# Cross-attention with text keys on one core: the loads of x move from SyncE's queue to GpSimd's

## The chip, the cores and the metric

One core of a Trainium2 chip runs the whole kernel. Time is device microseconds of one execution, lower is better; verdicts compare medians of several runs of both kernels on one chip. The engines are TensorE (PE, its weight loads shown as PEld), VectorE (DVE), ScalarE (ACT), GpSimd (POOL) and SyncE (SP), which here only issues DMAs.

## The reference

Every batch of 512 queries attends over 77 text keys, with 20 heads of 32 columns. The other three attentions of the module (object, others, image prompt) get slices of the keys that are empty for a context of 77 rows, so only the text part counts, all in float32:

```python
q = _heads(hidden_states @ to_q_w)                       # x: (32, 512, 640)
h_txt = _sdpa(q, _heads(ehs_txt @ to_k_w), _heads(ehs_txt @ to_v_w))
out = _merge(h_txt) @ to_out_w + to_out_b + hidden_states
```

where `_sdpa` is softmax(q kT / sqrt(32)) v for each head.

## The kernel before

Each float32 operand of a matmul is kept as a rounded high part and a low part, and each product is done as three passes (high x high, high x low, low x high). A first stage (some 280 us) makes keys and values of all batches and puts them into DRAM (`k_dram`, `v_dram`). Then 32 batches are worked through, each in five **slots** (`slot`, L557; n = 5 b + j): slot j takes head group j, four heads, 128 columns. The order in which each engine issues its instructions is the order in which the code calls them; nothing is rescheduled. So a call's place in `slot` is its place in its engine's queue.

What a slot does, with the lines that matter below:

- Scores, in four parts of 128 queries (L368 on PE), then the negated maxima (`nm`, L376 on DVE) and the exponentials with their sums (L386 on ACT).
- `normalize` (L401, POOL) scales the P of the slot before by `rs`, the reciprocal of the sums (L396, DVE). `transpose_p` (L408, DVE) turns it in blocks into `z`, and four stores (L415, SP) put it into a DRAM scratch, `pd`. `load_p` (L424 and L425, SP) reads a `pd` back as `raw`, in the layout that PE needs; there are three slots from a slot's scores to its values.
- `cast_p`, `rest_p` and `last_p` split `raw` into `pp`: L432 and L438 on ACT, L439 on DVE, L446 on POOL. `values` (L460, eight matmuls on PE) then makes P V; its last two matmuls read the rows that L446 writes. `split_a` (L104 on ACT, L105 on DVE) splits the result.
- Queries of the next slot (L333, PE), split by `split_q` (L344 and L348 on ACT, L350 on DVE).
- Pieces of the output projection of the batch before or the one before that (L490, PE). Residual rows are loaded by `load_residual` (L479, SP), get the bias by `add_bias` (L483, POOL), and `finish` (L518 on DVE, L522 on SP) adds and stores them.
- `refill` loads keys and values of a later head group (L310, L313 and L320, SP).

**x.** `load_x` (L262) loads x of a batch into the one buffer `xs`, in four quarters; quarter q goes to partitions 32 q to 32 q + 31, each as 32 partitions x 16 runs of 160 numbers (640 B), 320 KB in all. `transpose_x` (L273, DVE) turns `xs` in place, in four parts, and each part needs all four quarters. `split_x` (L280 on ACT, L281 on POOL) makes the five `xt` tiles of the next batch's queries. Slot j = 4 of batch b loads x of batch b + 2, slots 0 to 2 of batch b + 1 transpose it, slots 2 and 3 split it. The tables that place the parts hold, for each j, three tuples, which `slot` runs ahead of the queries' second half, behind the last scores, and at the end:

```python
TRANSPOSE_X = {0: ((), (0,), ()), 1: ((1,), (2,), ()), 2: ((3,), (), ())}
SPLIT_X = {2: ((0,), (1,)), 3: ((2, 3), (4,))}
```

All DMAs are issued by SP. Each of them waits, by the program's own counters, until the DMA issued eight places before on that queue has landed, besides what its data need.

Of the kernel before, what the change touches and what calls it, by code (L numbers as in the profile page):

```python
# [24 lines left out]
Q = 32  # L25
# [25 lines left out]
def kernel(  # L51
# [25 lines left out]
    nc = tc.nc  # L77
    B, S, C = x.shape
# [180 lines left out]

    xts, raws, pps, ats, xss, pds, sms, pqs, pas, xrs, pos = ({} for _ in range(11))  # L260

    def load_x(b, quarters=range(4)):  # L262

        if b not in xss:
            xss[b] = main.tile([P, S // Q, C // 4], F32, tag="xs", name="xs")
        xs = xss[b]
        src = x[b].rearrange("(a j) (q u) -> q j a u", j=Q, q=4)
        for q in quarters:
            nc.sync.dma_start(xs[q * Q : (q + 1) * Q, :, :], src[q])

    def transpose_x(b, i):
        part = xss[b][:, 4 * i : 4 * i + 4, :].rearrange("p a u -> p (a u)")
# [81 lines left out]
    def scores(n, t):  # L354
        b, j = divmod(n, NC_)
        g = GROUP_OF[j]
        qt, (kb, kc) = qts[n % 2], kbs[g]
        jg = j - GROUPS[g][0]
        sc = ps.tile([P, S], F32, tag="sc", name="sc", bufs=3)
        half = KCOLS // 2  # L360
        for m, (cols, keys_) in enumerate(
            (
                (slice(0, KCOLS), kb[:, jg]),
                (slice(0, half), kc[:, jg, 0]),
                (slice(half, KCOLS), kc[:, jg, 1]),
            )
        ):
            nc.tensor.matmul(  # L368
                sc[:, cols],
                qt[:, m, t * P : (t + 1) * P],  # L370
                keys_,
                start=(m == 0),
                stop=(m == 2),
            )
        nm = main.tile([P, HPC], F32, tag="nm", name="nm", bufs=3)
        nc.vector.tensor_reduce(  # L376
            nm, sc[:, :KCOLS].rearrange("p (h k) -> p h k", k=NKEY), AX.X, ALU.max, negate=True
        )
        return sc, nm

    def exps(n, t, sc, nm):
        if t == 0:
            sms[n] = main.tile([P, NQ * HPC], F32, tag="sm", name="sm", bufs=2)
        for i in range(HPC):
            at = t * HPC + i
            nc.scalar.activation(  # L386
                pnb[n % 2][:, at, :NKEY],
                sc[:, i * NKEY : (i + 1) * NKEY],
                AF.Exp,
                bias=nm[:, i : i + 1],  # L390
                accum_out=sms[n][:, at : at + 1],
            )

    def sums(n):
        rs = main.tile([P, NQ * HPC], F32, tag="rs", name="rs", bufs=2)
        nc.vector.reciprocal(rs, sms.pop(n))  # L396
        return rs

    def normalize(n, rs):
        pf = pnb[n % 2][:, :, :NKEY]  # L400
        nc.gpsimd.tensor_tensor(  # L401
            pf, pf, rs.unsqueeze(2).to_broadcast([P, NQ * HPC, NKEY]), ALU.mult
        )
# [24 lines left out]
    def cast_p(n):  # L428

        raw = raws[n]  # L430
        pp = late[0].tile([P, 5, S], FPR, tag="pp", name="pp", bufs=1)
        nc.scalar.copy(pp[:, 0:2, :], raw[:, 0:2, :])  # L432
        pps[n] = pp

    def rest_p(n):

        raw, pp = raws[n], pps[n]
        nc.scalar.copy(pp[:64, 4, :], raw[:64, 2, :])  # L438
        nc.vector.tensor_tensor(  # L439
            pp[:, 2:4, :], raw[:, 0:2, :], pp[:, 0:2, :].bitcast(F32), ALU.subtract  # L440
        )

    def last_p(n):

        raw, pp = raws.pop(n), pps[n]
        nc.gpsimd.tensor_tensor(  # L446
            pp[64:, 4, :], raw[:64, 2, :], pp[:64, 4, :].bitcast(F32), ALU.subtract
        )
# [33 lines left out]
    def add_bias(b, t):  # L482
        nc.gpsimd.tensor_tensor(xrs[b, t], xrs[b, t], bias, ALU.add)  # L483
# [49 lines left out]
    PIECES = {2: (1, 0), 3: (1, 2), 4: (1, 4), 0: (2, 6), 1: (2, 8)}  # L533
    RESIDUAL = {1: (1, 0), 2: (1, 1), 3: (1, 2), 4: (1, 3)}
    BIAS = {2: (1, 0), 3: (1, 1), 4: (1, 2), 0: (2, 3)}
    TRANSPOSE_X = {0: ((), (0,), ()), 1: ((1,), (2,), ()), 2: ((3,), (), ())}
    SPLIT_X = {2: ((0,), (1,)), 3: ((2, 3), (4,))}
    wos = []

    def take(m):  # L540
        values(m)
        split_a(m)

    def refill(b, j, part):

        heads = range(2 * part, 2 * part + 2)
        segments = SEGMENTS[4 * part : 4 * part + 4]
        if j == 0:
            load_keys(b, 1, heads)
        elif j == 1:  # L550
            load_values(b, 0, segments)
        elif j == 2 and b + 1 < B:
            load_keys(b + 1, 0, heads)
        elif j == 3:
            load_values(b, 1, segments)

    def slot(n, beside=None):  # L557
        b, j = divmod(n, NC_)
        ahead, more = n + 1 < N, b + 1 < B
        back, first = PIECES[j]  # L560
        bo_, has_out = b - back, b >= back
        xsplits = SPLIT_X.get(j, ((), ())) if more else ((), ())
        turns = TRANSPOSE_X.get(j, ((), (), ())) if more else ((), (), ())
        taken, second = takes.get(n), seconds.get(n)

        refill(b, j, 0)
        if taken is not None:
            cast_p(taken)
        s = scores(n, 0)
        if taken is not None:  # L570
            rest_p(taken)
        if n:
            normalize(n - 1, sums(n - 1))
        if taken is not None:
            last_p(taken)
        exps(n, 0, *s)
        if ahead:
            queries(n + 1, 0, 2)
        s = scores(n, 1)
        if n - LAG + 1 in pds and n > LATE:  # L580
            load_p(n - LAG + 1)
        refill(b, j, 1)
        finish()
        if j == 4 and b + 2 < B:
            load_x(b + 2, (0, 1))
        if j in RESIDUAL and b >= RESIDUAL[j][0]:
            load_residual(b - RESIDUAL[j][0], RESIDUAL[j][1])
        if j in BIAS and b >= BIAS[j][0]:
            add_bias(b - BIAS[j][0], BIAS[j][1])
        exps(n, 1, *s)  # L590
        for i in turns[0]:
            transpose_x(b + 1, i)
        if ahead:
            queries(n + 1, 2, NC_)
        s = scores(n, 2)
        if n:
            transpose_p(n - 1)
        if ahead:
            split_q(n + 1)
        exps(n, 2, *s)  # L600
        if j == 4 and b + 2 < B:
            load_x(b + 2, (2, 3))
        for c in xsplits[0]:
            split_x(b + 1, c)
        if has_out:
            piece(bo_, first)
        if taken is not None:
            values(taken)
        if beside:
            beside()  # L610
        s = scores(n, 3)
        finish()
        for i in turns[1]:
            transpose_x(b + 1, i)
        if taken is not None:
            split_a(taken)
        for c in xsplits[1]:
            split_x(b + 1, c)
        exps(n, 3, *s)
        if has_out:  # L620
            piece(bo_, first + 1)
        for i in turns[2]:
            transpose_x(b + 1, i)
        if second is not None:
            cast_p(second)
            rest_p(second)
            last_p(second)
            take(second)
            if second + 2 in pds and second + 2 not in takes.values():
                load_p(second + 2)  # L630
# [66 lines left out]

    with tc.manual_schedule(engines=ENGINES):
        g0, gn = GROUPS_KV[-1]
        load_x(0)  # L700
        load_keys(0, 0)
        for h in range(2):
            context_values(g0, gn, 0, h, psv)
        for i in range(NQ):
            transpose_x(0, i)
        for c in range(NC_):
            split_x(0, c, nc.gpsimd if c % 2 else nc.vector)
        load_x(1)
        for t0 in (P, 2 * P):
            for h in range(2):  # L710
                context_values(g0, gn, t0, h, psv)
        queries(0, 0, NC_)
        split_q(0)
        for n in range(LATE):
            slot(n, (lambda: context_values(g0, gn, 3 * P, n // 2, psv)) if n % 2 else None)
        psv.release()
        kvp.release()
        late.append(ctx.enter_context(tc.tile_pool(name="late", bufs=1, reuse_waits="tile")))
        late.append(
            ctx.enter_context(tc.tile_pool(name="psl", bufs=1, space=PSUM, reuse_waits="tile"))  # L720
        )
        load_p(0)
        load_p(1)
        wos.append(late[0].tile([P, NC_, 2, C], FPR, name="wo_s"))
        for n in range(LATE, LATE + 4):
            slot(n)
            for k in {LATE: (0, 1), LATE + 1: (2, 3), LATE + 2: (4,)}.get(n, ()):
                nc.sync.dma_start(wos[0][:, k].bitcast(F32), wo_dram[:, k].bitcast(F32))
        for n in range(LATE + 4, N):
            slot(n)  # L730
        end()
# [40 lines left out]
```

## Time and profile before

| what | us |
|---|---|
| median of 3 runs (lowest, highest) | 2010.02 (2009.55, 2010.04) |
| the profiled execution | 1996.0 |
| its span | 1994.2 |
| DMA, moved in the span | 423.54 MB, mean 212 GB/s |
| POOL L401, 160 times | 364.4 busy, 2277 ns each |
| POOL L446, 160 times | 209.4 busy, 1309 ns each |
| DVE L273, 128 times | 106.5 busy, 834 ns each |
| loads of x, 128 of 320 KB | 7.0 from issue to landing (median) |

The page's parts are read in this order: busy time and span, then what each engine waits for, then the timelines of a stretch. A wait is told as "engine tile line <- releaser": total us, number of times, longest. In a timeline each line has start, duration, engine, source line, operation and tiles (out<-in); the number in brackets is the engine's idle time before it and what ended it. PE's granted clock is 1.00 in every 100 us window from 450 us on, so a slot's length there is PE's own work and its waits. The timelines below are from 1014 to 1048 us, in the middle of the run; a slot j = 0 starts there at 1024.2 and the next at 1034.5.

### The profile page before, as it was taken

Reading aid. Unit: us, or ns where it says so; the run is one execution under the profiler, and the core shown is the slowest. Engines: PE = TensorE matmul, PEld = TensorE weight load, DVE = VectorE, ACT = ScalarE, POOL = GpSimd, SP = SyncE. Lnnn points to the kernel's source line nnn. Section 1 sums busy time; section 2 is a strip of 40 time slices with the busy share of each in tenths; the row PEclk is TensorE's granted clock in tenths of the full one; section 3 lists DMA queues with packets and bytes.
Section 4 is the critical chain, followed back from the end, with each engine's and each line's share of the span. In section 5 each row is a group of like instructions: output and inputs, shape, how many; then the busy total and the mean of one; then the engine's idle time right before and its main releaser. Section 6 shows DMA issues by size and latency. Waiting matters only on the chain.

```text
span 1994.2 us, 38184 instructions
## 1 busy us (share of the span) xinstructions
PE 1950.5 (98%) x11012; PEld 1760.0 (88%) x11012; DVE 1352.5 (68%) x2159; ACT 1598.2 (80%) x6377; POOL 982.8 (49%) x617
## 2 busy tenths in 40 slices
PE   8999997899999999999999999999999999999998
PEld 7889986788899999899899898999989898988997
DVE  4443225777777777777777777777777777777774
ACT  3321128899999999999899999999999899998993
POOL 0000023555555555655556655566655566555554
PEclk9999998999999999999999999999999999999999
DMA  7994366889988889898988899998888888888975
GB/s 172 225 261 107 106 148 146 232 213 232 226 225 226 229 221 231 216 229 212 232 225 224 220 225 230 229 233 222 219 223 223 223 223 225 224 218 230 228 198 164
DMA packets 555997, 423.54 MB, mean 212 GB/s; under 512 B 170192, under 2 KB 459502, under 8 KB 555790
## 3 DMA queue, kind: packets, MB, share of 16 engines
q1 hardware_dynamic: 555789, 421.10, 83.9%
q8 instruction: 91, 1.49, 0.3%
q14 instruction: 117, 0.95, 0.2%
HBM read 245.61 MB, written 175.32 MB: 211 GB/s over the span
## 4 chain that ended last, share of the span: by engine, by line
PE 78%; DMA 9%; SPq 4%; POOL 3%; ACT 2%; issue 2%; DVE 2%; DVEq 0%; ACTq 0%; POOLq 0%
PE po L490 24%; PE pq L333 24%; PE pa L460 13%; PE sc L368 9%; PE pv L197 4%; PE pk L168 4%; DMA raw<-pd 3%; POOL pn L401 2%; DMA pd<-z 2%; SPq L114 1%; DMA xs<-in_x_dram 1%; POOL pp L446 1%; ACT pn L386 1%; DMA k_dram<-ks 1%; DMA cs<-in_ctx_dram 1%
## 5 line engine op out<-in xcount | busy, mean ns | idle before, releaser
L386 ACT ACTIVATE pn<-sc,nm 128x77 f32<-128x77 f32 x2560 | 802.0, 330 | 44.6 <-DVE nm L376 33.8
L401 POOL TENSOR_TENSOR pn<-pn,rs 128x1232 f32<-128x1232 f32 x160 | 364.4, 2277 | 670.3 <-DVE rs L396 643.9
L490 PE MATMUL po<-wo_s,at 128*128 128x320 f32 x3840 | 626.9, 312 | 2.2 <-DVE xr L518 2.2
L333 PE MATMUL pq<-xt,wq_s 128*128 128x512 f32 x2400 | 622.4, 400 | 0.0
L490 PEld LDWEIGHTS po<-wo_s,at 128*128 128x128 f32 x3840 | 566.3, 189 | 2.7 <-DVE xr L518 2.5
L386 ACT ACTIVATION_READ_ACCUMULATOR pn<-sc,nm 128x1 f32 x2560 | 533.1, 208 | 0.0
L333 PEld LDWEIGHTS pq<-xt,wq_s 128*128 128x128 f32 x2400 | 429.6, 190 | 77.4 <-POOL xt L281 0.2
L376 DVE TENSOR_REDUCE nm<-sc 128x4 f32<-128x308 f32 x640 | 294.6, 460 | 298.2 <-PE sc L368 291.0
L460 PE MATMUL pa<-pp,vb 128*128 128x512 f32 x1280 | 334.9, 402 | 18.4 <-ACT pp L432 9.8
L460 PEld LDWEIGHTS pa<-pp,vb 128*128 128x128 f32 x1280 | 243.5, 198 | 62.8 <-POOL pp L446 14.3
L408 DVE STREAM_TRANSPOSE z<-pn 128x1280 f32<-128x1280 f32 x160 | 241.5, 1509 | 36.2 <-POOL pn L401 31.6
L439 DVE TENSOR_TENSOR pp<-raw,pp 128x1024 fp32r<-128x1024 f32 x160 | 196.1, 1226 | 82.4 <-ACT pp L432 72.2
L368 PEld LDWEIGHTS sc<-kc,qt 128*128 128x128 f32 x1280 | 212.8, 189 | 27.2 <-ACT qt L348 4.2
L446 POOL TENSOR_TENSOR pp<-raw,pp 64x512 fp32r<-64x512 f32 x160 | 209.4, 1309 | 37.0 <-ACT pp L438 19.8
L368 PE MATMUL sc<-kc,qt 128*128 128x154 f32 x1280 | 222.9, 255 | 4.5 <-DVE qt L350 3.9
L350 DVE TENSOR_TENSOR qt<-pq,qt 64x512 fp32r<-64x512 f32 x320 | 214.3, 670 | 7.5 <-ACT qt L344 3.1
L281 POOL TENSOR_TENSOR xt<-xs,xt 128x512 fp32r<-128x512 f32 x157 | 200.0, 1296 | 19.4 <-ACT xt L280 12.5
L483 POOL TENSOR_TENSOR xr<-xr,bias 128x640 f32<-128x640 f32 x128 | 201.3, 1573 | 9.7
L348 ACT CAST qt<-qt 64x512 fp32r<-64x512 f32 x320 | 198.8, 621 | 8.9
L368 PE MATMUL sc<-kb,qt 128*128 128x308 f32 x640 | 196.1, 306 | 1.2 <-ACT qt L344 1.2
L432 ACT CAST pp<-raw 128x1024 fp32r<-128x1024 f32 x160 | 170.1, 1063 | 29.7 <-DMA raw<-pd 28.9
L104 ACT CAST at<-pa 128x512 fp32r<-128x512 f32 x160 | 94.9, 593 | 82.2 <-PE pa L460 81.1
(41 smaller groups left out, 1530.8 us busy)
## 6 DMA issues: line engine op xcount, KB each, us to landing
pd<-z SPq DMA_DIRECT2D x640, 160.0 KB, 3.6
raw<-pd SPq DMA_DIRECT2D x160, 512.0 KB, 4.3
xs<-in_x_dram SPq DMA_DIRECT2D x128, 320.0 KB, 7.0
xr<-in_x_dram SPq DMA_DIRECT2D x128, 320.0 KB, 3.8
out_dram<-xr SPq DMA_DIRECT2D x128, 320.0 KB, 3.2
raw<-pd SPq DMA_DIRECT2D x160, 128.0 KB, 4.4
v_dram<-vs SPq DMA_DIRECT2D x19, 640.0 KB, 4.0
k_dram<-ks SPq DMA_DIRECT2D x80, 128.0 KB, 2.4
```

The lines of the kernel that those rows point to most:

```text
L281: engine.tensor_tensor(parts[1], src, parts[0].bitcast(F32), ALU.subtract)
L333: nc.tensor.matmul(pqs[n], wq_s[:, k, a, j * P : (j + 1) * P], xts[b, k][:, c, :], start=(k == 0 and m == 0), stop=(k == NC_ - 1 and m == 2),)
L350: nc.vector.tensor_tensor(qt[r, 1 + w, :], pq[r], qt[r, 0, :].bitcast(F32), ALU.subtract)
L368: nc.tensor.matmul(sc[:, cols], qt[:, m, t * P : (t + 1) * P], keys_, start=(m == 0), stop=(m == 2),)
L376: nc.vector.tensor_reduce(nm, sc[:, :KCOLS].rearrange("p (h k) -> p h k", k=NKEY), AX.X, ALU.max, negate=True)
L386: nc.scalar.activation(pnb[n % 2][:, at, :NKEY], sc[:, i * NKEY : (i + 1) * NKEY], AF.Exp, bias=nm[:, i : i + 1], accum_out=sms[n][:, at : ...
L401: nc.gpsimd.tensor_tensor(pf, pf, rs.unsqueeze(2).to_broadcast([P, NQ * HPC, NKEY]), ALU.mult)
L408: nc.vector.transpose(z.rearrange("p b t j -> p t b j"), pn.rearrange("p (t h) k -> p t (h k)", t=NQ).rearrange("p t (b i) -> p t b i", i=Q),)
L446: nc.gpsimd.tensor_tensor(pp[64:, 4, :], raw[:64, 2, :], pp[:64, 4, :].bitcast(F32), ALU.subtract)
L460: nc.tensor.matmul(pas[n], vb[:, t, :, a], pp[:, c, :], start=(m == 0), stop=(m == len(PASSES) - 1),)
L483: nc.gpsimd.tensor_tensor(xrs[b, t], xrs[b, t], bias, ALU.add)
L490: nc.tensor.matmul(pos[b, t, h][:, :HALF], ats[b * NC_ + j][:, a, t * P : (t + 1) * P], wos[0][:, j, c, h * HALF : (h + 1) * HALF], start= ...
```

## The change

The four quarters of x are issued by POOL (`nc.gpsimd`) in place of SP; only the loads of the first two batches stay on SP. Quarter 0 is issued in slot j = 4 behind `last_p`, quarters 1 and 2 in the same slot behind `add_bias`, quarter 3 in slot j = 0 of the next batch behind `last_p`. Before, quarters 0 and 1 were issued ahead of the residual's load of slot 4, and 2 and 3 behind the third part's exponentials. The first of the four transpositions of x moves from behind the last scores of slot 0 to its end, on DVE from ahead of `split_a`'s L105 to behind it. The computation is the same.

```diff
-    def load_x(b, quarters=range(4)):
+    def load_x(b, quarters=range(4), engine=nc.gpsimd):
...
         for q in quarters:
-            nc.sync.dma_start(xs[q * Q : (q + 1) * Q, :, :], src[q])
+            engine.dma_start(xs[q * Q : (q + 1) * Q, :, :], src[q])
...
-    TRANSPOSE_X = {0: ((), (0,), ()), 1: ((1,), (2,), ()), 2: ((3,), (), ())}
+    TRANSPOSE_X = {0: ((), (), (0,)), 1: ((1,), (2,), ()), 2: ((3,), (), ())}
...
         if taken is not None:
             last_p(taken)
+        if j == 4 and b + 2 < B:
+            load_x(b + 2, (0,))
+        elif j == 0 and b and b + 1 < B:
+            load_x(b + 1, (3,))
         exps(n, 0, *s)
...
         finish()
-        if j == 4 and b + 2 < B:
-            load_x(b + 2, (0, 1))
         if j in RESIDUAL and b >= RESIDUAL[j][0]:
             load_residual(b - RESIDUAL[j][0], RESIDUAL[j][1])
         if j in BIAS and b >= BIAS[j][0]:
             add_bias(b - BIAS[j][0], BIAS[j][1])
+        if j == 4 and b + 2 < B:
+            load_x(b + 2, (1, 2))
         exps(n, 1, *s)
...
         exps(n, 2, *s)
-        if j == 4 and b + 2 < B:
-            load_x(b + 2, (2, 3))
         for c in xsplits[0]:
...
-        load_x(0)
+        load_x(0, engine=nc.sync)
...
-        load_x(1)
+        load_x(1, engine=nc.sync)
```

## The prediction

> **What bounds the kernel now.** First the page's totals.
>
> ```profile
> span 1994.2 us, 38184 instructions
> PE 1950.5 (98%) x11012; PEld 1760.0 (88%) x11012; DVE 1352.5 (68%) x2159; ACT 1598.2 (80%) x6377; POOL 982.8 (49%) x617
> ```
>
> TensorE (PE) is busy 98% of the span, and in the timeline of PE a slot (one head group of one batch) takes 10.3 us, five slots a batch. A change of queues can't shorten a slot whose PE never waits; it can only remove or add PE waits. So the second view is that of PE's waits from 450 to 1900 us, and of its weight loads (PEld):
>
> ```profile
> PE pa L460 <- POOL pp L446: 4.8, 8, 1.5
> PEld pa L460 <- POOL pp L446: 9.9, 13, 2.0
> ```
>
> In total us, times, longest: there is one wait left, that of the attention-times-values matmuls (L460) for `last_p` on POOL (L446). Measured from slot start to slot start, the slots that hold it are late by about 7 us in all: between the 4.8 of idle matmuls and the 9.9 of idle loads. I use 7. They are all slots j = 1. Why there, the timeline of SP's queue shows, for the end of a slot j = 4 and the slot j = 0 that starts at 1024.2:
>
> ```profile
> 1017.70 1.07 SPq L269 DMA_DIRECT2D xs<-in_x_dram  x2
> 1020.83 2.41 SPq L415 DMA_DIRECT2D pd<-z  x4
> 1023.29 1.89 SPq L269 DMA_DIRECT2D xs<-in_x_dram  x2
> 1028.30 0.39 SPq L424 DMA_DIRECT2D raw<-pd  x1
> 1029.54 0.47 SPq L425 DMA_DIRECT2D raw<-pd  x1
> 1031.04 0.30 SPq L310 DMA_DIRECT2D kb<-k_dram  x1
> ```
>
> Start, duration. Two quarters of x stand ahead of the stores of P (pd), two behind; then the load that slot j = 1 needs (raw) goes out at 1028.30 and 1029.54, the second only when a quarter of x has landed. SP's own waits from 450 to 1900 us put a number on that:
>
> ```profile
> SPq L425 <- DMA xs<-in_x_dram: 24.0, 26, 2.1
> ```
>
> 26 times in some 28 batches SP stands still until x lands, with raw's second part behind it. So x on SP's queue is what makes `raw` late.
>
> **What leaves SP.** Four L269 issues a batch, of 0.54 us (median, below), 30 batches. Those 2.1 us of SP lie beside PE's work and are worth nothing; the wait above is what counts. With x off the queue pd goes out with nothing of x ahead, and raw right when pd has landed. In this batch raw needed to land some 0.2 us earlier for no stall, in the worst 1.5 to 2.0; x ahead costs pd the transfer of two quarters (in the start-up, one quarter after another lands every 1.1 to 1.7 us), so 2 to 3 us come back. I credit all 7 us; the bounds are 0 (x still takes the same DMA engines) and 9.9.
>
> The Trainium skill (DMA: Bandwidth & Descriptors, Issuing engines are not separate DMA queues) speaks against any credit: DMAs of all issuers share 16 engines, and a second issuer saves only the issue time. The 24.0 us of L425 are waits for a landing and not issue time, so I follow the row; by the rule the forecast below would be 7 us longer.
>
> **What POOL gets.** Four DMA issues a batch. POOL's timeline, from slot j = 4 to j = 1:
>
> ```profile
> 1020.71 1.58 POOL L483 TENSOR_TENSOR xr<-xr,bias 128x640 f32<-128x640 f32 x1
> 1026.97 2.28 POOL L401 TENSOR_TENSOR pn<-pn,rs 128x1232 f32<-128x1232 f32 x1 [4.67 <-DVE rs L396]
> 1029.32 1.30 POOL L446 TENSOR_TENSOR pp<-raw,pp 64x512 fp32r<-64x512 f32 x1
> 1030.70 1.58 POOL L483 TENSOR_TENSOR xr<-xr,bias 128x640 f32<-128x640 f32 x1
> 1037.65 2.28 POOL L401 TENSOR_TENSOR pn<-pn,rs 128x1232 f32<-128x1232 f32 x1 [5.38 <-DVE rs L396]
> 1040.02 1.29 POOL L446 TENSOR_TENSOR pp<-raw,pp 64x512 fp32r<-64x512 f32 x1
> ```
>
> In brackets the idle time before an instruction. Quarter 0 goes ahead of the L483 of slot 4, quarters 1 and 2 behind it: three issues in 4.67 us of idle time. Quarter 3 goes behind L446 of slot 0, with 5.38 us free. They wait for nothing themselves: xs is free once the last split of slot 3 (POOL's own L281) is done. Behind them stand L483, wanted by L518 a slot later, and L401. What POOL takes for one issue, X, no row shows. A quarter is 32 partitions x 16 runs of 640 B, 512 runs. From below: SP's 0.5. From above: POOL walks the 512 elements a partition of L446 in 1.3 us; if runs cost as much as elements, and both the reading and the writing side are walked, 2.6. I take 1.3, one walk: 3 x 1.3 = 3.9 fits into 4.67, and costs nothing. Without that cover (X over 1.56) L401, then L446 of slot 0 come late; L446 ends at 1030.62 and the seventh of the eight L460 matmuls, the first that reads its rows, is at 1030.51 + 6 x 0.234 = 1031.9. So 1.3 us more are free, and PE stalls from X = (4.67 + 1.3) / 3 = 2.0 on.
>
> The Trainium skill (same page, Latency and other measured facts) gives the first byte about 1 us for an issue from GpSimd and 0.6 from SP. No row here shows the first; by it X would be about 0.5 + 0.4 and fit as well.
>
> **What is late next: quarter 3.** Before, it went out by 1025.2, 8.7 us ahead of the transposition of x that needs all four (L273, on DVE). Now it goes out at 1030.65, when L446 of slot 0 has ended. In exchange that transposition moves behind L105, to the end of the slot. DVE's timeline there:
>
> ```profile
> 1033.83 0.83 DVE L273 STREAM_TRANSPOSE xs<-xs 128x640 f32<-128x640 f32 x1
> 1034.59 0.65 DVE L105 TENSOR_TENSOR at<-pa,at 128x512 fp32r<-128x512 f32 x1
> 1035.16 0.46 DVE L376 TENSOR_REDUCE nm<-sc 128x4 f32<-128x308 f32 x1
> 1036.12 1.23 DVE L439 TENSOR_TENSOR pp<-raw,pp 128x1024 fp32r<-128x1024 f32 x1 [0.50 <-ACT pp L432]
> 1037.27 0.24 DVE L396 RECIPROCAL rs<-sm 128x16 f32<-128x16 f32 x1
> ```
>
> Swapping L273 and L105 costs nothing by itself. But behind L273 stand L376, L439 and L396 of slot 1, and L396 releases L401, L401 goes ahead of L446, and L446 releases PE:
>
> ```profile
> 1040.84 2.04 PE L460 MATMUL pa<-pp,vb 128*128 128x512 f32 x8
> ```
>
> Counted back: the seventh matmul is at 1040.84 + 1.41 = 1042.25. L446 (1.3) and L401 (2.28), with 0.1 between, put L401 at 1038.5 at the latest; it starts 0.38 after L396, so L396 at 1038.15; L439 1.15 before, 1037.0; L376 0.55 before, 1036.45; L273 0.8 before, 1035.65. Quarter 3 has 1035.65 - 1030.65 = 5.0 us from the start of its issue to its landing. The same transfers on SP (all uses of xs):
>
> ```profile
> L269 SPq DMA_DIRECT2D xs<-in_x_dram x128: 316/536/2149, 268.2 to 1853.6; - x128
> DMA to landing us min/median/max: 4.0/7.0/9.2
> ```
>
> First ns of one issue (min/median/max), then us to landing. At 4.0 (the start-up, nothing ahead) it is in time; at 7.0 it is 2.0 late, at 9.2 4.2 late. The median holds quarters behind quarters, and quarter 3 now goes alone; but it goes beside the four pd stores of slot 0 (640 KB), and its issue takes X - 0.5 = 0.8 longer. The nearest row is the first quarter of a batch in slots j = 4, alone behind raw: median 5.7 in the trace. I take 5.7: 0.7 us late, in each of 30 batches, 21 us.
>
> **Sum**, against the profiled execution of 1996.0 us (span 1994.2, 1.8 around it): 1996 - 7 + 21 = 2010. The median of the runs shown, 2010.02, is 0.70% above that execution, so the forecast is 2010 x 1.0070 = 2024 us, 0.7% slower. Bounds in the same scale: from 5.0 us and less (no stall) to 7.0 us for the landing (60 us lost), 2003 to 2063; a little room on the low side gives 2012 to 2065 as the range of this case alone.
>
> **The rivals.**
> - In time. Quarter 3 lands within 5.0 us, as it does in the start-up rows; the stalls of slot 1 go: 1989 in the profile, 2003 us. For it: pd is short and sent early in slot 0 once SP is free. Against: the DMA engines run at shares of 1.0 to 1.2 in the 2 us windows around slot 0, and 0.8 us or so of issue is added.
> - POOL's issue is long, X = 2.6. L401 of slot 0 is 3 x 2.6 - 4.67 = 3.1 late, PE stalls 3.1 - 1.3 = 1.8; quarter 3 goes 3.1 later and takes 5.7 + 1.3, lands at 1040.75 against 1035.65 + 1.8: 3.3 more. 5.1 x 30 = 153, less 7: 2142, so 2157 us. It decides from X = 2.0 on. For it: 512 runs on two sides, and no row of POOL issuing anything; against: 1.3 us for 512 elements a partition, with arithmetic.
> - The change doesn't do what it says. x takes the same engines at the same time, raw stays as late, and quarter 3 is just in time: 2010 us, within 0.2%.
>
> **How the numbers follow.** Quarter 3 late 0.42, in time 0.27, long issue 0.20, no change 0.11. 0.2% (4 us) is about what a measurement tells from no change. Faster 0.28 (in time, and a little of no change), same 0.11, slower 0.61. The range reaches from 2000 (in time, and all 9.9 us of waits gone) to 2100 (X of 2.3), which leaves out the long issues above and a little below.
>
> **What would show it.** POOL's rows of L269: X itself. DVE's idle time before L273, released by DMA xs, 0.7 us or so each batch, and PE L460 waiting for POOL L446 in slot 1, about 20 us in all. SP's waits for xs gone, and `raw` issued some 2 us earlier in slot 0. It is wrong if L273 never waits (then 2003), or if POOL's L401 in slot 0 has no idle time left before it (then over 2060).

## The result, and the profile after

The changed kernel is slower: 2020.10 us, median of 9 runs (2015.81 to 2029.61), beside 2009.55 us for the kernel before (9 runs); the ratio of the means (2020.8 and 2006.7) is 1.0070, 95% interval 1.0053 to 1.0088. That of the two medians is 1.0052, as the runs of the kernel before spread from 1994.61 to 2012.01. By the 2% bound of the verdicts that is "same"; the interval is well clear of 1. The forecast was 2024 us and 0.7%.

The profiled execution took 2018.62 us, that of the kernel before 1996.0, near the low end of its runs; so the two profiles lie further apart (22.6 us) than the means (14.1). Its page, first the totals and then the DMA queues (packets, MB, share of 16 engines):

```profile
span 2016.8 us, 38335 instructions
PE 1958.4 (97%) x11012; PEld 1762.5 (87%) x11012; DVE 1352.4 (67%) x2159; ACT 1589.6 (79%) x6377; POOL 1054.8 (52%) x737
...
q1 hardware_dynamic: 492429, 381.77, 72.8%
q0 software_dynamic: 11520, 39.33, 8.0%
```

The span grew by 22.6 us while PE's instructions stayed the same. POOL has 120 instructions more, the DMA issues, and is busy 72 us longer. The waits between 450 and 1900 us (total us, times, longest) show where the span grew:

```profile
DVE xs L273 <- DMA xs<-in_x_dram: 60.3, 28, 3.7
...
PEld pa L460 <- POOL pp L446: 28.3, 27, 2.6
PE pa L460 <- POOL pp L446: 16.8, 24, 2.1
...
ACT pp L432 <- DMA raw<-pd: 3.4, 3, 2.1
```

DVE waits for x before the first transposition in every batch, which it never did before in this stretch. PE's one wait is still that for L446, more than three times as long as before (4.8). And what caused it before, ACT's wait for `raw`, is nearly gone (3.4 us); in the kernel before the same view had

```profile
ACT pp L432 <- DMA raw<-pd: 27.4, 24, 2.2
```

One late load was exchanged for another. The chain of waits of the changed kernel shows one batch of it (start, duration, what):

```profile
1043.77 0.59 POOL pp L446
1044.36 0.66 issue
1045.02 6.35 DMA xs<-in_x_dram
...
1051.49 0.09 DVE xs L273
...
1052.26 0.44 DVE nm L376
1052.70 1.06 DVE pp L439
1053.77 0.24 DVE rs L396
...
1054.14 2.28 POOL pn L401
...
1056.49 1.28 POOL pp L446
...
1057.82 0.74 PE pa L460 x2
```

("issue" is time in which the engine waited for nothing that the profile shows.) Quarter 3 is issued when L446 of slot 0 is done, lands 6.35 us later, and L273, L376, L439, L396, L401 and L446 follow one upon another, up to the last two matmuls of L460 in slot 1. POOL's timeline of the same batch:

```profile
1033.78 1.29 POOL L446 TENSOR_TENSOR pp<-raw,pp 64x512 fp32r<-64x512 f32 x1
1035.02 0.67 POOL L269 DMA_DIRECT2D xs<-in_x_dram  x1
1035.76 1.56 POOL L483 TENSOR_TENSOR xr<-xr,bias 128x640 f32<-128x640 f32 x1
1037.26 1.29 POOL L269 DMA_DIRECT2D xs<-in_x_dram  x2
1041.41 2.28 POOL L401 TENSOR_TENSOR pn<-pn,rs 128x1232 f32<-128x1232 f32 x1 [2.87 <-DVE rs L396]
```

One issue takes POOL 0.67 us. L401 of slot 0 still has 2.87 of its 4.67 us of idle time left, so POOL is no bound there.

Slot by slot (from one slot's first matmul to the next's, all five kinds take 10.31 to 10.34 us if nothing waits), the slots j = 1 from the eleventh slot to the end lost 26.5 us, against 8.8 before: 17.7 more, and no other kind of slot changed by 1 us. The rest of the 22.6 lies mostly ahead: 3.9 us before the first slot, where the program is the same, and 1.4 in the first ten slots (0.4 in the other slots, and the end is 0.7 shorter). "Lost" below is this sum over the 29 slots j = 1 of batches 2 to 30 (counted from 0). It tells more than the whole time: the eleventh slot begins anywhere from 400.6 to 411.7 us in the twelve traces.

### The profile page after: what moved, and what is told of

Its sections match the earlier page's. It is cut to its first block, busy times and chain, and to the rows that moved or that the text cites. A ratio compares the mean times of both kernels' runs of the same rounds, so it can differ in the third digit from the quotient of the medians.

```text
span 2016.8 us, 38335 instructions
## 1 busy us (share of the span) xinstructions
PE 1958.4 (97%) x11012; PEld 1762.5 (87%) x11012; DVE 1352.4 (67%) x2159; ACT 1589.6 (79%) x6377; POOL 1054.8 (52%) x737
## 3 DMA queue, kind: packets, MB, share of 16 engines
q1 hardware_dynamic: 492429, 381.77, 72.8%
q0 software_dynamic: 11520, 39.33, 8.0%
## 4 chain that ended last, share of the span: by engine, by line
PE 63%; DMA 12%; POOL 6%; ACT 5%; issue 4%; DVE 3%; SPq 1%; DVEq 0%; POOLq 0%; ACTq 0%
PE po L490 19%; PE pq L333 18%; PE pa L460 10%; PE sc L368 7%; DMA raw<-pd 4%; PE pv L197 4%; PE pk L168 4%; POOL pn L401 4%; DMA pd<-z 3%; DMA xs<-in_x_dram 3%; POOL pp L446 2%; ACT pn L386 2%; DVE pp L439 1%; DVE nm L376 1%; ACT pp L432 1%
## 5 line engine op out<-in xcount | busy, mean ns | idle before, releaser
L401 POOL TENSOR_TENSOR pn<-pn,rs 128x1232 f32<-128x1232 f32 x160 | 364.2, 2276 | 624.8 <-DVE rs L396 403.3
L376 DVE TENSOR_REDUCE nm<-sc 128x4 f32<-128x308 f32 x640 | 292.9, 458 | 283.9 <-PE sc L368 278.4
L460 PE MATMUL pa<-pp,vb 128*128 128x512 f32 x1280 | 338.7, 402 | 33.6 <-POOL pp L446 20.3
L460 PEld LDWEIGHTS pa<-pp,vb 128*128 128x128 f32 x1280 | 242.3, 197 | 83.4 <-POOL pp L446 34.0
L368 PEld LDWEIGHTS sc<-kc,qt 128*128 128x128 f32 x1280 | 212.8, 189 | 26.5 <-ACT qt L348 4.2
L439 DVE TENSOR_TENSOR pp<-raw,pp 128x1024 fp32r<-128x1024 f32 x160 | 196.4, 1227 | 44.9 <-ACT pp L432 40.8
L446 POOL TENSOR_TENSOR pp<-raw,pp 64x512 fp32r<-64x512 f32 x160 | 208.5, 1303 | 33.6 <-ACT pp L438 21.5
L281 POOL TENSOR_TENSOR xt<-xs,xt 128x512 fp32r<-128x512 f32 x157 | 199.5, 1297 | 17.7 <-ACT xt L280 13.1
L483 POOL TENSOR_TENSOR xr<-xr,bias 128x640 f32<-128x640 f32 x128 | 201.1, 1572 | 8.7
```

What stands on the lines that cost most here:

```text
L368: nc.tensor.matmul(sc[:, cols], qt[:, m, t * P : (t + 1) * P], keys_, start=(m == 0), stop=(m == 2),)
L376: nc.vector.tensor_reduce(nm, sc[:, :KCOLS].rearrange("p (h k) -> p h k", k=NKEY), AX.X, ALU.max, negate=True)
L401: nc.gpsimd.tensor_tensor(pf, pf, rs.unsqueeze(2).to_broadcast([P, NQ * HPC, NKEY]), ALU.mult)
L439: nc.vector.tensor_tensor(pp[:, 2:4, :], raw[:, 0:2, :], pp[:, 0:2, :].bitcast(F32), ALU.subtract)
L446: nc.gpsimd.tensor_tensor(pp[64:, 4, :], raw[:64, 2, :], pp[:64, 4, :].bitcast(F32), ALU.subtract)
L460: nc.tensor.matmul(pas[n], vb[:, t, :, a], pp[:, c, :], start=(m == 0), stop=(m == len(PASSES) - 1),)
```

## The experiments

All but two of the ten differ from the changed kernel in where x's quarters are issued, by whom, or both. Medians of one trace each, over the loads of x for batches 5 to 30, in us from the start of slot 0 of the batch before; `raw` is its first part (L424), 512 of 640 KB. Ratios are against the kernel before:

| kernel | issuer | quarter 3 issued | landed | raw landed | lost, us | ratio (95%) |
|---|---|---|---|---|---|---|
| before | SP | -0.1 | 7.6 | 11.5 | 8.8 | |
| changed | POOL | 6.4 | 12.4 | 9.8 | 26.5 | 1.0070 (1.0053 to 1.0088) |
| e1 | POOL | -0.1 | 8.7 | 11.6 | 9.5 | 1.0001 (0.9983 to 1.0020) |
| e2 | POOL | 5.0 | 12.0 | 10.3 | 20.0 | 1.0074 (1.0048 to 1.0101) |
| e3 | POOL | 8.0 | 12.9 | 9.8 | 47.7 | 1.0205 (1.0177 to 1.0233) |
| e4 | SP | 3.7 | 8.3 | 10.1 | 0.6 | 0.9951 (0.9932 to 0.9969) |
| e5 | SP | 0.2 | 7.5 | 11.5 | 10.3 | 0.9989 (0.9970 to 1.0008) |
| e6 | POOL | 6.4 | 12.3 | 9.8 | 54.6 | 1.0216 (1.0190 to 1.0242) |
| e9 | SP | 7.2 | 11.6 | 8.2 | 11.7 | 1.0011 (0.9996 to 1.0027) |
| e10 | POOL | -1.2 | 5.7 | 10.2 | 4.5 | 0.9962 (0.9946 to 0.9978) |
| e11 | SP (0 to 2: POOL) | 8.4 | 12.7 | 9.7 | 41.5 | 1.0190 (1.0165 to 1.0216) |
| e12 | POOL (0 to 2: SP) | 6.4 | 11.6 | 8.4 | 7.4 | 0.9982 (0.9966 to 0.9998) |

**e1: quarter 3 already in slot 4.**

```diff
-        elif j == 0 and b and b + 1 < B:
-            load_x(b + 1, (3,))
...
         if j == 4 and b + 2 < B:
-            load_x(b + 2, (1, 2))
+            load_x(b + 2, (1, 2, 3))
```

> The changed kernel, but quarter 3 of x is issued by GpSimd in slot j=4 behind quarters 1 and 2, some 6 us earlier. Theory (quarter 3 lands too late for DVE's L273, and that alone makes the loss): L273 never waits, PE's waits for L446 fall from 26 us to under 4, below the kernel before too since x is off SP's queue; ratio to the kernel before 0.996 (0.994 to 0.999), against 1.007 for the change. Rival A (the four issues on GpSimd themselves cost, wherever they stand): as many issues, so the ratio stays near 1.007. Rival B (x's transfers hold up the loads of P as before, whoever issues them): L273 doesn't wait but raw lands late again, ratio 1.000 to 1.003.

Measured: 1.0001, rival B. L273 no longer waits (no wait for x between 450 and 1900 us), but ACT's wait for `raw` is back, and with it PE's:

```profile
ACT pp L432 <- DMA raw<-pd: 32.2, 26, 2.2
PEld pa L460 <- POOL pp L446: 11.2, 17, 1.3
```

So quarter 3's lateness is the loss, and rival A falls: with as many issues on POOL the 0.7% is gone. But x off SP's queue did not free `raw`. Its first part was issued at 3.8 us of slot 0, 0.9 earlier than before the change, its second at 4.3, 2.0 earlier, and both landed as late as before (11.6 and 11.9): quarters 1 to 3 landed at 4.7, 6.8 and 8.7, beside it.

**e2: quarter 3 ahead of L446.**

```diff
             normalize(n - 1, sums(n - 1))
+        if j == 0 and b and b + 1 < B:
+            load_x(b + 1, (3,))
         if taken is not None:
             last_p(taken)
...
-        elif j == 0 and b and b + 1 < B:
-            load_x(b + 1, (3,))
```

> The changed kernel, but quarter 3 is issued in slot j=0 between L401 and L446, so 1.4 us earlier, and L446 comes 0.7 us later (it has 1.3 us to spare). Theory: it lands about 11.0 us after the slot's start, against 12.4 now and 11.5 needed; the loss per batch falls from 0.9 to about 0.15 us, ratio 0.998 (0.996 to 1.001). Rival A: L446 is later, nothing is saved, ratio 1.007 or more. Rival B: ratio 1.003 or more.

Measured: 1.0074, the theory's size is missed. Issued 1.4 us earlier, quarter 3 landed only 0.3 earlier: it took 7.1 us and not 6.0, perhaps since it now went beside more of `raw`. The lost time did fall a little, from 26.5 to 20.0 us, which the ratio can't tell apart. The ratio alone would suit rival A too; but the slots j = 0, where L446 now stands behind the issue, are as long as before (10.31), so a later L446 cost nothing.

**e3: quarter 3 behind L483.**

```diff
-        elif j == 0 and b and b + 1 < B:
-            load_x(b + 1, (3,))
...
             load_x(b + 2, (1, 2))
+        elif j == 0 and b and b + 1 < B:
+            load_x(b + 1, (3,))
```

> The changed kernel, but quarter 3 is issued in slot j=0 behind add_bias (L483), 1.6 us later. Theory: each of 30 batches loses 1.6 us more, 47 us, ratio 1.030 (1.024 to 1.034), DVE's wait before L273 grows by about as much. Rival A: as many issues on GpSimd, ratio 1.007. Rival B: 1.007 to 1.010.

Measured: 1.0205, between. Issued 1.6 us later it landed 0.6 later (4.9 us on its way). The direction is the theory's; how late an issue makes the landing was taken wrongly, nearly three times too steep. What holds in all three is the step from landing to loss: landed at 12.0, 12.4 and 12.9, lost per slot 0.69, 0.91 and 1.64. The forecast had counted back that it must land by 11.45. Taken batch by batch, what lies beyond 11.45 adds up to 19.9, 25.8 and 46.0 us in these three traces, close to the 20.0, 26.5 and 47.7 lost; in e9, e11 and e12 below to 12.1, 38.9 and 8.8, against 11.7, 41.5 and 7.4.

**e4: the new places, all on SP.**

```diff
-    def load_x(b, quarters=range(4), engine=nc.gpsimd):
+    def load_x(b, quarters=range(4), engine=nc.sync):
```

> The changed kernel with its new places, but all loads of x issued by SP. Theory: quarter 3 goes out a few us earlier, since SP isn't held by L446 of slot 0, so L273 doesn't wait; but quarters stand ahead of raw on SP's queue again, so raw is late as before the change: ratio 0.999 to 1.005, PE's waits for L446 8 us or more. Rival A (the issues on GpSimd cost): ratio 1.000 or less, PE's waits at most those of the kernel before.

Measured: 0.9951, faster than both kernels. That is below the theory's range and within rival A's, which e1 had ruled out as it stood. PE's waits are gone; the windows view of 450 to 1900 us (us, busy time and count of PE, PEld, DVE, ACT, POOL, clock, DMA share, GB/s) has PE without a gap:

```profile
450.00:1900.00 1450.00, 1450.00 (x8291) 1314.38 (x8290) 1090.01 (x1743) 1333.73 (x5477) 855.58 (x533) 1.00 0.88 225
```

In the kernel before that figure for PE is 1445.22, in the changed one 1433.08. SP, which waits for neither L401 nor L446, issued quarter 0 at 1.7 us of slot 4 where POOL came to it at 6.7, 1 and 2 at 3.9 and 4.3 (8.9 and 9.6), and quarter 3 at 3.7 us of slot 0 (6.4). `raw`, although behind x on the same queue, landed at 10.1, in time. Two readings were left: that it matters when x moves, or that issuing on POOL holds up SP's loads by itself.

**e10: GpSimd, as early as it can.**

```diff
+        if j == 4 and b + 2 < B:
+            load_x(b + 2, (0, 1))
         if n:
             normalize(n - 1, sums(n - 1))
         if taken is not None:
             last_p(taken)
         if j == 4 and b + 2 < B:
-            load_x(b + 2, (0,))
-        elif j == 0 and b and b + 1 < B:
-            load_x(b + 1, (3,))
+            load_x(b + 2, (2,))
...
-            load_x(b + 2, (1, 2))
+            load_x(b + 2, (3,))
```

> All four quarters issued by GpSimd in slot j=4, as early as its order allows: 0 and 1 ahead of L401 (in 1.4 us of idle time), 2 behind L446, 3 behind L483. Nearest on GpSimd to the places that SP had in e4. Theory 2 (it matters when x moves, not who issues it): x is out of the way of slot 0's raw, raw lands 10.5 us or sooner after the start of slot 0, ratio 0.995 to 0.998. Rival (issuing on GpSimd holds up SP's loads by itself, as e1 at 1.0001 against e4 at 0.9951 could also be read): raw lands at 11.5 as in e1, ratio 1.000 or more.

Measured: 0.9962, theory 2. With all issues on POOL the kernel is faster than before, and not to be told from e4 (it loses 1.4 us more in slots j = 0, outside the table). `raw` is in time, and PE hardly waits between 450 and 1900 us:

```profile
PEld pa L460 <- POOL pp L446: 3.2, 4, 1.1
ACT pp L432 <- DMA raw<-pd: 2.6, 4, 1.9
```

How long `raw` was on its way, from issue to landing, says the same in all these traces. It took 8.0 us in e1, with quarters 1 to 3 beside it; 6.5 in the kernel before and 6.3 in the changed one; 5.4 in e4, with quarter 3 alone; and 4.1 to 4.2 in e10 and in e9 and e12 below, where at least quarters 0 to 2 had landed when it was issued. Of these, e10 has x on POOL and e9 on SP.

**e9: SP, but quarter 3 late.** As e4, with quarter 3 in the place that it has in e3.

> As e4 (all x on SP, spread), but quarter 3 is issued behind the second half of refill of slot j=0, so behind raw on SP's queue, at 5.5 to 6.5 us after the slot's start, about when GpSimd issued it in the changed kernel (6.4). Theory 2: it lands about as late as there, 11.5 to 12.5, L273 waits, ratio 0.999 to 1.005. Rival (GpSimd's transfers take longer on their way): it lands by 10.5, no wait, ratio 0.995 as e4.

Measured: 1.0011, within theory 2's range. But SP came to the issue only at 7.2 us, later than planned, and the way was 4.4 us, so the late landing does not rule out the rival; e11 and e12 look at it. What e9 shows is that on SP too a quarter 3 that lands at 11.6 makes DVE wait, and takes away what e4 gains:

```profile
DVE xs L273 <- DMA xs<-in_x_dram: 40.0, 27, 2.6
```

**e12 and e11: one part on each queue.** In e12 quarters 0 to 2 are given `nc.sync` in the changed kernel; in e11 quarter 3 alone, behind `add_bias` of slot 0.

> The changed kernel with quarters 0 to 2 issued by SP in the same places of the code (so 5 us earlier, since SP isn't held by L446), and quarter 3 still by GpSimd at 6.4 us of slot j=0. Theory 2 (what counts is the work ahead in the DMA engines at that moment, not the issuer): with quarters 1 and 2 long landed, quarter 3 takes 4.5 us and not 6.0, lands at 10.8 to 11.3, hardly any wait; ratio 0.995 to 1.000. Rival (a transfer issued by GpSimd takes some 6 us by itself): it lands at 12.3, ratio 1.004 to 1.008.

> The changed kernel with quarter 3 alone issued by SP, behind the second half of refill of slot j=0, at 6 to 7.5 us of the slot; quarters 0 to 2 by GpSimd as in the change. Theory 2: quarters 1 and 2 still lie in the DMA engines beside raw; quarter 3 lands at 12 to 13, L273 waits, ratio 1.004 to 1.012. Rival: issued by SP it takes 4.5 us whatever lies ahead, lands at 11 to 11.5, ratio 1.002 or less.

Measured: 0.9982 for e12. With the other quarters landed by 1.9 us of slot 0 and not by 6.7, the same issue by POOL at 6.4 us took 5.2 us, not 6.0; it landed at 11.6, later than theory 2's 11.3 and earlier than the rival's 12.3. Measured for e11: 1.0190, well above both expectations: SP came to quarter 3 only at 8.4 us, behind waits for other loads and stores. On its way it took 4.3 us, 0.6 less than POOL's in e3 (4.9, issued at 8.0); in e9 it took 4.4, 0.8 less than POOL's in e12 (5.2, issued at 6.4). So there may be some part of the rival too, at most 0.6 to 0.8 us of a way of 5 to 6. Of that, 0.2 to 0.35 is the issue itself (0.67 us against SP's 0.44 and 0.32 there), and SP's issues were 0.4 and 0.8 us later, which by e2 and e3 shortens the way by itself.

**e5: the kernel before, with only the transposition moved.**

```diff
-    TRANSPOSE_X = {0: ((), (0,), ()), 1: ((1,), (2,), ()), 2: ((3,), (), ())}
+    TRANSPOSE_X = {0: ((), (), (0,)), 1: ((1,), (2,), ()), 2: ((3,), (), ())}
```

> The kernel before with nothing but the first transposition of x moved to the end of slot j=0, behind L105. Theory: the limit there is raw, not L105 or L273; ratio 1.000 (0.998 to 1.002). Rival (the move itself costs, since L273 now stands between slot 1's start and its L376): ratio 1.003 or more.

Measured: 0.9989, interval across 1: the move by itself does nothing that can be measured.

**e6: the changed kernel with the transposition in its old place** (the same line of the table, the other way).

> The changed kernel with the first transposition of x in its old place, ahead of L105 in slot j=0. Theory (L273 waits for quarter 3, and what stands behind it is late): L105 (0.65 us) is now behind the wait too, so some 0.6 us a batch more, 19 us, ratio 1.016 (1.011 to 1.020). Rival (the loss isn't DVE's wait): ratio 1.007.

Measured: 1.0216, the theory's direction and more than its size. The median slot j = 1 is 0.7 us longer than in the changed kernel, about as expected; the mean is 0.97 longer, by some slots that lose up to 6 us. Why those few are so long was not tried. So the move of L273 belongs to the change: without it the late quarter costs about twice as much.

## Why the prediction was right

- *The place.* PE's only wait from 450 to 1900 us is L460 for L446 in slots j = 1: so it is in both kernels.
- *POOL's issue, taken as 1.3 us.* It is 0.67, near the lower bound. It fitted, so the size had no effect, and the rival of the long issue is out. The forecast named 0.8 us that the longer issue would add to quarter 3's way and then left it out of the sum; as the issue took 0.67 and not 1.3, that did no harm.
- *Quarter 3, taken as 5.7 us from issue to landing, 0.7 late.* 6.0 in the median, landed at 12.4 against 11.45: 0.9 late, and 0.91 lost in each slot j = 1. The rows that the 5.7 was taken from, the first quarters in slots j = 4, have a median of 6.0 in the trace; with that the term would have been 30 us. The count back along L273, L376, L439, L396, L401, L446 was right to a tenth or two, and e2, e3, e9, e11 and e12 confirm it at other landings (the sums beyond 11.45 above). The term of 21 us measured 26.5.
- *The credit of 7 us for leaving SP's queue.* This step was wrong in its reason. `raw` did land earlier, by 1.7 us, close to the 2 us forecast. But being off SP's queue does not do that by itself: in e1 x is off it, `raw` goes out sooner and lands as late as ever; in e4 x is on it and `raw` is in time. In the changed kernel quarter 3 was moved out of its way as well. What decides in these traces is how much of x is on its way while `raw` is: 4.1 us with next to none, 8.0 with three quarters. The forecast set the Trainium skill's rule aside (DMA: Bandwidth & Descriptors, Issuing engines are not separate DMA queues: DMAs of all issuers share the 16 engines); e1 and e4 are on the rule's side. The wait that L425 showed (24.0 us) was real, but taking it away gained nothing: in e1 raw's second part was issued 2.0 us sooner and landed no sooner.
- *The sum.* 14 us more were forecast, 17.7 more were lost in slots j = 1, and 22.6 lie between two profiled executions, of which 3.9 ahead of any changed instruction. That the ratios agree to the digit is partly luck, as is the sum: the credit never shows as such, since a slot can't be held up by `raw` and by quarter 3 both; the later one alone decides. So the old loss (7, measured as 8.8) gives way to the new one (21, measured as 26.5) whether `raw` gets earlier or not. The range of this case alone should have begun at the 2003 us that the bounds gave, and not at 2012; the measured time lies in both.
- *The rivals.* "In time" is what e4 and e10 do, at 0.995 and 0.996, where the forecast had 2003 us (0.9965). "The change doesn't do what it says" is what e1 does, at 1.0001.

## What to carry to other kernels

When a load moves, count two deadlines: that of the load itself, back through every engine up to the bound one, and that of the loads which it will now run beside. An issue time is no landing time: here an issue 1.4 us earlier landed 0.3 earlier, and one 1.6 later 0.6 later, so take the landing from a run. And an engine that has work in order ahead of the issue, as POOL has L401 and L446, issues late; here SP issued from the same lines of code some 5 us sooner (quarter 3: 2.7), and between these two kernels lie 0.7% lost and 0.5% won.

## What the runs showed of the hardware

- POOL was held 0.65 to 0.67 us by one issue of 512 runs of 640 B (0.81 at most), next to SP's 0.32 at least and 0.54 in the median (2.15 at most, in the kernel before).
- The same quarter went out as 96 packets of 3.4 KB from POOL (11,520 for 120) and as 528 from SP (63,360 fewer in its queue). That fewer packets save time of the DMA engines is not shown: by the queues' shares (72.8% and 8.0% after, 83.9% before) all transfers took 1630 us of all 16 engines after and 1673 before, but 1637 in e9 with all of x on SP, and 1622 to 1642 in the traces with all of it on POOL.
- Quarter 3 took from 4.3 (e11) to 8.7 us (e1) from issue to landing in the medians. Moving its issue 1.4 us earlier or 1.6 later moved its landing by 0.3 and 0.6.
